# Moving the sums of two convolution tiles behind the normalised pieces of the next layer's input

## The chip, the core and the metric

The kernel runs on one core of a Trainium2 chip. The metric is the device time of one execution in microseconds (us), as a median of several runs. The engines are named as in the profile: PE (matrix multiplications; PEld is its loading of weights), DVE (vector), ACT (scalar and activation), POOL (general purpose) and SP (here it only issues DMAs). Each engine works off its own queue in order; an instruction whose input isn't there yet holds up all that stand behind it on its engine.

## The reference, cut to what matters

Eight images of 32x32 positions ("tokens", 1024 per image) with 256 channels, all in float32. The first layer adds to each image a 3x3 convolution (192 output channels) beside a small attention with relative positions (64 channels). The second layer is a full attention over the 1024 tokens, then a mixture-of-experts layer.

```python
x = x + _L0_conv_ref(_gn(x), ...)        # conv 3x3 -> 192 channels, attention -> 64 channels
t = _to_tokens(x)
t = t + _L1_attn_ref(_ln_t(t), ...)      # _ln_t normalises each token: (v - m) / sqrt(s + eps)
t = t + _L1_ffn_ref(_ln_t(t), ...)
```

What matters here are the sums that the convolution adds to `x`, and the adds `t + ...` and normalised pieces `_ln_t(t)` at the start of the second layer.

## The kernel before, in words

The images go one after the other through the first two stages: `conv_layer_attention(b, ...)` is the first layer's attention of image b, `attention_layer(b, ...)` the second layer's. The mixture of experts follows for all images at the end and isn't touched. An image lies in SBUF as `T[b]`, 128 partitions by 8 pieces of tokens (NT = 8) by 256 channels.

**The convolution** is computed by a short-filter transform: DVE makes six differences `gdif` of the normalised image, PE multiplies them with six transformed filters `convw`, and sums of the products give four neighbouring output columns. `conv_steps` (L517) is a generator: one step is one matmul at L531; 12 steps make a tile `pc` of PSUM with a pair of products; there are three pairs for each of two halves of the image, so 72 steps and six tiles per image. At the end of a tile ACT copies `pc` to SBUF (`m`, L540, two buffers), and POOL turns the pair into sums and adds them to `T`: pair 0 takes two adds into `sd` (L546, L547) and two adds into `T` (L550, L554); pair 1 has, besides, two multiplications on ACT, of one half of `sd` by 2 (L549) and of `sd` by 4 (L552); pair 2 is a single add (L543).

**The seam** is the start of `attention_layer(b)`, where the second layer of image b begins and the first layer of image b+1 is prepared. It normalises the eight pieces of image b in two groups of four (q = 0, 1). Per piece, DVE makes `n` (L815, two buffers), PE transposes it twice into `tpn` (L819), and POOL adds `n` to `T[b]` (L820); n's buffer is free again when both have read it. Between the pieces `fill` takes steps of `input_steps(b+1)`, the next image's projections: its small matmuls `prel` (L484) of 32 rows, the copies of those by DVE (L496) and ACT (L498), and its transposes `tpw` (L509), copied by ACT (L513) and DVE (L511). Each of these steps also names a number of convolution steps, which `conv.run` issues: four are run ahead of the seam and 20 in it, so exactly two tiles, pair 0 and pair 1 of the first half, end in a seam. In POOL's order the first tile's sums stand between the adds of the first and the second piece, the second tile's between those of the sixth and the seventh. After a group, ACT copies the transposes to `nT` (L823). Then come the second layer's projections `pq` (L834), its scores and the rest; POOL adds the bias `bo` to the whole of `T[b]` (L928) after the second tile of scores, and L919 is the first to read that.

There are seven seams with a convolution in them (image 1 to 7 as next image); in the last image's there is none. Image 0's whole convolution runs in `conv_layer_attention`.

**Order.** `tc.manual_schedule` fixes the order of PE and POOL to the program's order in this part. The order on ACT, DVE and SP is set by the scheduler, which places instructions by their estimated times, the program's order breaking ties; so an instruction can stand in ACT's queue at another place than in the program's text.

```python
conv.run(products)                 # in fill(), between the pieces
...
fill(1000.0)                       # all steps that are left
conv.whole()                       # fill up a tile that has been begun
```

Of the kernel before, what the change touches and what calls it, by code (L numbers as in the profile page):

```python
# [10 lines left out]
FP = mybir.dt.float32  # L11
I32 = mybir.dt.int32
AF = mybir.ActivationFunctionType
ALU = mybir.AluOpType
# [3 lines left out]
P = 128  # L18
# [7 lines left out]
CO = C - DK  # L26
# [10 lines left out]
def kernel(  # L37
# [26 lines left out]
    nc = tc.nc  # L64
# [27 lines left out]
    with ExitStack() as ph:  # L92
        wp = ph.enter_context(tc.tile_pool(name="wp", bufs=1))
        work = ph.enter_context(tc.tile_pool(name="work", bufs=1))
# [38 lines left out]
        def st_tile(name):  # L133
            return ps_st["st"].tile([P, 512], FP, tag="st", name=name)
# [80 lines left out]
        def f_tile(name):  # L215
            return work.tile([P, 2, 4, 512], FP, tag="F", name=name, bufs=3)
# [184 lines left out]
        def input_steps(b, held):  # L401
# [112 lines left out]
                yield 0.86, 0  # L514
            held["units"] = [Unit(0, kq, rh, rwd)]

        def conv_steps(b, place):  # L517

            n = 3 * KC
            for r in range(2):
                four = T[b][:, 4 * r : 4 * r + 4, 0:CO]
                for pair in range(3):
                    pc = place[0]("pc")[:, 0 : 2 * CO].rearrange("p (v o) -> p v o", v=2)
                    for v in range(2):
                        for i in range(n):
                            dy, kc = divmod(i, KC)
                            at = (16 * r + dy) * NQ  # L530
                            nc.tensor.matmul(  # L531
                                pc[:, v, :],
                                lhsT=gflat[:, 2 * pair + v, kc, at : at + P],
                                rhs=convw[:, 2 * pair + v, dy, kc * CO : (kc + 1) * CO],
                                start=i == 0,
                                stop=i == n - 1,
                            )
                            if v and i == n - 1:
                                m = work.tile([P, 2, CO], FP, tag="m", name="m", bufs=2)
                                nc.scalar.copy(m, pc)  # L540
                                add = nc.gpsimd.tensor_tensor
                                if pair == 2:
                                    add(four[:, 0:4:3], four[:, 0:4:3], m, ALU.add)  # L543
                                else:
                                    sd = work.tile([P, 2, CO], FP, tag="sd", name="sd")
                                    add(sd[:, 0], m[:, 0], m[:, 1], ALU.add)  # L546
                                    add(sd[:, 1], m[:, 0], m[:, 1], ALU.subtract)  # L547
                                    if pair:
                                        nc.scalar.mul(sd[:, 1], sd[:, 1], 2.0)  # L549
                                    add(four[:, 0:2], four[:, 0:2], sd, ALU.add)  # L550
                                    if pair:
                                        nc.scalar.mul(m, sd, 4.0)  # L552
                                        sd = m
                                    add(four[:, 2:4], four[:, 2:4], sd, ALU.add)  # L554
                            yield

        class Unit:


            def __init__(self, n, kq, rh, rwd):  # L560
                self.g, self.half = divmod(n, 2)
                g, cols = self.g, slice(self.half * 512, self.half * 512 + 512)
                self.rh = rh[g][:, cols]


                self.F = f_tile("F")
                for a in range(2):
                    for hl in range(HG):
                        r = 32 * ((hl + 2 * a) % HG)
                        h = g * HG + hl  # L570
                        nc.sync.dma_start(
                            out=self.F[r : r + 16, a],
                            in_=rh[g][a * 64 + hl : a * 64 + 64 : HG, cols].unsqueeze(1).to_broadcast([16, 4, 512]),
                        )
                        nc.sync.dma_start(
                            out=self.F[r + 16 : r + 24, a],
                            in_=kq[DK + h * DH : DK + (h + 1) * DH, cols].unsqueeze(1).to_broadcast([DH, 4, 512]),
                        )
                for a in range(2):
                    for hl in range(HG):  # L580
                        r = 32 * ((hl + 2 * a) % HG)
                        nc.sync.dma_start(
                            out=self.F[r + 24 : r + 32, a],
                            in_=rwd[g].rearrange("(e j h) s -> h j e s", e=4, h=HG)[hl, :, :, cols],
                        )
                self.mx = work.tile([P, 4, HG], FP, tag="mx", name="mx", bufs=2)
                self.pts = {}
                self.po = None
# [88 lines left out]
            def settle(self, at):  # L677

                pa = st_tile("pa")
                for i in range(4):  # L680
                    nc.tensor.transpose(pa[:, i * P : (i + 1) * P], self.os[:, i * P : (i + 1) * P], ident)
                pav = pa.rearrange("p (i h c) -> p i h c", i=4, h=HG)
                rc = work.tile([P, 4, HG, 1], FP, tag="rc", name="rc", bufs=2)
                nc.vector.reciprocal(rc, pav[:, :, :, DH : DH + 1])
                nc.vector.tensor_tensor(
                    at[:, self.half * 4 : self.half * 4 + 4, self.g * 32 : self.g * 32 + 32].rearrange(
                        "p i (h d) -> p i h d", d=DH
                    ),
                    pav[:, :, :, 0:DH],
                    rc.to_broadcast([P, 4, HG, DH]),  # L690
                    ALU.mult,
                )
# [105 lines left out]
        def attention_layer(b, fill, conv, maxima):  # L798
# [24 lines left out]
                    nc.scalar.copy(nT[:, kc, q * 512 : (q + 1) * 512], tps[kc].rearrange("p j t -> p (j t)"))  # L823
            fill(1000.0)
            conv.whole()

            qkv = f_tile("qkv").rearrange("p a e s -> p (a e s)")
            qk = [qkv[:, i * S : (i + 1) * S] for i in range(2)]
# [116 lines left out]
            m = mv2[:, b]  # L945
# [33 lines left out]
        class Conv:  # L979


            def __init__(self, b):
                self.place = [po_tile]
                self.steps = conv_steps(b, self.place)
                self.left = 2 * NV * 3 * KC if b < B else 0

            def run(self, n):
                n = min(n, self.left)
                for _ in range(n):
                    next(self.steps)  # L990
                self.left -= n

            def whole(self):

                self.run(self.left % (6 * KC))
# [17 lines left out]
        with tc.manual_schedule(engines={mybir.EngineType.PE, mybir.EngineType.Pool}):  # L1013
            conv = Conv(0)
            means = []
            for b in range(B):
# [33 lines left out]
                conv = following  # L1050

                def fill(us):

                    while us > 0:
                        took, products = next(steps, (None, None))
                        if took is None:
                            break
                        us -= took
                        conv.run(products)

                def maxima(s):
                    if not last:
                        pair(held["units"], s, held["rwq"])

                means.append((b, *attention_layer(b, fill, conv, maxima)))
                del T[b]
            token_mean(*means.pop())
# [4 lines left out]
    work = ctx.enter_context(tc.tile_pool(name="fwork", bufs=2))  # L1072
# [21 lines left out]
    def sm(shape, name):  # L1094
        return small.tile(shape, FP, tag=name, name=name)
# [40 lines left out]
    for k in range(TOPK):  # L1136
        m = sm([B, 1], f"m{k}")
# [213 lines left out]
```

## Time and profile before

| | |
|---|---|
| median of 3 runs | 2393.74 us (2389.73 to 2403.38) |
| the profiled execution, its own time | 2405.51 us |
| its span in the profile | 2403.7 us |
| mean granted TensorE clock | 0.962 |
| PE busy | 2315.2 us (96%), 17273 instructions |
| DVE, ACT, POOL busy | 1474.8, 1028.8, 475.3 us |
| copy m (L540) | 48 times, 0.48 us |
| POOL adds L546 and L547 | 32 times each, 0.59 us |
| POOL adds L550 and L554 | 32 times each, 1.00 us |
| ACT multiplications L549 and L552 | 16 times each |
| POOL add of n (L820) | 64 times, 0.73 us |

How to read the views: a line of the timeline has the start in us from the span's begin, the length, the engine, the line of the kernel, the operation, the tiles (output <- inputs) with their shapes, and how many instructions are merged; in brackets stands the time that the engine sat idle before it and who released it. A line of the waits has who waited at which line, for whom, the us in total, the times and the longest. A line of a stretch has the stretch, its length, then the busy us and number of instructions of PE, PEld, DVE, ACT and POOL, then the granted TensorE clock (1.00 is full), the mean busy share of the DMA engines and their GB/s.

### The profile page before, as it was taken

The numbers are of one execution on the slowest core, as the hardware profiler recorded it, in microseconds if no ns is written. First come the engines' busy times: TensorE is split into PE (matmuls) and PEld (weight loads), VectorE is DVE, ScalarE is ACT, GpSimd is POOL, SyncE is SP. The second block draws the span as 40 slices with busy tenths as digits, with TensorE's granted clock in tenths as the row PEclk, the third lists the DMA queues.
The fourth block names the chain that finished last, engine by engine and source line by source line (L and its number), as shares of the span: only waits on it lengthen the run. The fifth ranks groups of instructions, "written<-read, shape, count | busy, mean of one in ns | idle before, by whom it ended". The sixth has DMA issues, their size and how long they took to land. (4 is left out here: it accounts for less than half of the span.)

```text
span 2403.7 us, 41841 instructions
## 1 busy us (share of the span) xinstructions
PE 2315.2 (96%) x17273; PEld 1326.5 (55%) x17273; DVE 1474.8 (61%) x2645; ACT 1028.8 (43%) x1717; POOL 475.3 (20%) x446
## 2 busy tenths in 40 slices
PE   6999999999999999999999999999998789999998
PEld 5535753664366436743773376347633556666665
DVE  7776487558756774677477737773773524444443
ACT  2355335434543463356326632663355322222332
POOL 3202130213021202210230023002301032222231
PEclk7999999899989998999899989998998989999999
DMA  3521252225122503250325033403430122122210
GB/s 107 100 44 30 39 101 37 42 37 102 25 52 38 104 12 58 36 108 3 59 54 91 3 58 73 72 6 55 79 48 2 58 88 70 70 71 71 83 48 27
DMA packets 71469, 135.84 MB, mean 57 GB/s; under 512 B 12000, under 2 KB 24168, under 8 KB 69232
## 3 DMA queue, kind: packets, MB, share of 16 engines
q1 hardware_dynamic: 65488, 115.47, 24.6%
q0 software_dynamic: 3056, 15.73, 2.0%
q8 instruction: 137, 2.24, 0.4%
q10 hardware_dynamic: 2736, 1.97, 0.3%
q14 instruction: 52, 0.43, 0.1%
HBM read 53.43 MB, written 25.17 MB: 33 GB/s over the span
## 5 line engine op out<-in xcount | busy, mean ns | idle before, releaser
L607 DVE TENSOR_REDUCE my<-lg 128x32 f32<-128x1024 f32 x512 | 617.3, 1222 | 173.2 <-PE st L639 125.8
L647 ACT ACTIVATE PT<-st 128x512 f32<-128x512 f32 (+1 forms) x944 | 541.5, 633 | 306.6 <-PE st L639 302.2
L639 PE MATMUL st<-F,km 32*128 32x512 f32 x2048 | 546.4, 643 | 14.2 <-DMA F<-mb 8.9
L599 PE MATMUL lg<-km,F 24*128 24x512 f32 x2048 | 503.6, 636 | 1.8 <-DMA F<-kq 1.8
L656 PE MATMUL po<-PT,vall 128*32 128x256 f32 (+1 forms) x3200 | 315.6, 454 | 2.4 <-ACT PT L647 2.4
L531 PE MATMUL pc<-convw,gdif 128*128 128x192 f32 x1152 | 249.6, 363 | 0.7 <-ACT convw L296 0.7
L656 PEld LDWEIGHTS po<-PT,vall 128*32 128x32 f32 x3200 | 67.0, 108 | 314.9 <-issue 281.7
L599 PEld LDWEIGHTS lg<-km,F 24*128 24x128 f32 x2048 | 143.8, 183 | 163.6 <-issue 124.3
L531 PEld LDWEIGHTS pc<-convw,gdif 128*128 128x128 f32 x1152 | 202.8, 206 | 55.8 <-issue 31.1
L639 PEld LDWEIGHTS st<-F,km 32*128 32x128 f32 x2048 | 178.0, 184 | 92.1 <-issue 48.3
L1281 PE MATMUL py<-w,hT 128*128 128x256 f32 x1024 | 223.6, 379 | 0.0
L1264 PE MATMUL phd<-n2T,w 128*128 128x512 f32 x512 | 223.6, 594 | 0.0
L1281 PEld LDWEIGHTS py<-w,hT 128*128 128x128 f32 x1024 | 194.6, 190 | 33.3 <-issue 7.7
L327 POOL TENSOR_TENSOR T<-T,l0b 128x2048 f32<-128x2048 f32 x8 | 36.3, 4539 | 628.8 <-PE tpx L320 628.8
L1264 PEld LDWEIGHTS phd<-n2T,w 128*128 128x128 f32 x512 | 97.0, 191 | 114.8 <-issue 107.6
L1288 DVE TENSOR_TENSOR r<-py,n 128x256 f32<-128x256 f32 x64 | 27.1, 424 | 213.2 <-PE py L1281 213.1
L1271 ACT ACTIVATE hT<-phd,b1c 128x512 f32<-128x512 f32 x128 | 86.3, 686 | 96.3 <-PE phd L1264 96.1
L872 PE MATMUL lg<-qkv 128*128 128x512 f32 x256 | 121.1, 595 | 0.0
L881 DVE TENSOR_REDUCE nm<-lg 128x1 f32<-128x1024 f32 x64 | 78.1, 1221 | 67.5 <-PE lg L872 67.5
L903 PE MATMUL po<-pt,qkv 128*128 128x256 f32 x512 | 116.5, 380 | 0.0
L820 POOL TENSOR_TENSOR T<-T,n 128x256 f32<-128x256 f32 x64 | 47.3, 755 | 344.1 <-DVE n L815 344.1
L903 PEld LDWEIGHTS po<-pt,qkv 128*128 128x128 f32 x512 | 96.7, 190 | 28.4 <-issue 11.0
(250 smaller groups left out, 2594.7 us busy)
## 6 DMA issues: line engine op xcount, KB each, us to landing
F<-rh SPq DMA_DIRECT2D x256, 128.0 KB
F<-kq SPq DMA_DIRECT2D x256, 64.0 KB
F<-rwd SPq DMA_DIRECT2D x256, 64.0 KB
w<-in_L_ffn_W_dram SPq DMA_DIRECT2D x32, 512.0 KB
rwd<-rw SPq DMA_DIRECT2D x16, 512.0 KB
Td<-T POOLq DMA_DIRECT2D x8, 1024.0 KB, 4.2
T<-Td SPq DMA_DIRECT2D x8, 1024.0 KB
out_dram<-yo SPq DMA_DIRECT2D x16, 512.0 KB
```

What stands on the lines that cost most here:

```text
L531: nc.tensor.matmul(pc[:, v, :], lhsT=gflat[:, 2 * pair + v, kc, at : at + P], rhs=convw[:, 2 * pair + v, dy, kc * CO : (kc + 1) * CO], sta ...
L599: nc.tensor.matmul(lg[:, a, :], lhsT=self.F[r : r + 24, a, 0, i * P : (i + 1) * P], rhs=KM[self.g][r : r + 24, a].rearrange("p e k -> p (e ...
L607: nc.vector.tensor_reduce(my[:, :, hl], lg.rearrange("p a (y x) -> p y a x", y=WW), AX.XY, ALU.max)
L639: nc.tensor.matmul(st[:, i, :] if len(heads) > 1 else st, lhsT=KM[self.g][r : r + 32, a, e, :], rhs=self.F[r : r + 32, a, e, :], start=Tru ...
L647: nc.scalar.activation(self.pts[j][:, hs, :], st, AF.Exp)
L656: nc.tensor.matmul(self.po[32 * hl : 32 * hl + 32, cols], lhsT=vall[:, j, h * (DH + 1) : h * (DH + 1) + 32], rhs=self.pts[j][:, hl, cols], ...
L872: nc.tensor.matmul(lg[:, h, :], lhsT=qk[0][:, i * P : (i + 1) * P], rhs=qk[1][:, h * 512 : (h + 1) * 512], start=True, stop=True,)
L881: nc.vector.tensor_reduce(nm, lg, AX.X, ALU.max, negate=True)
L903: nc.tensor.matmul(po[:, 0:IB], lhsT=v1[:, jc, :], rhs=pt[:, jc, :], start=jc == 0, stop=jc == NT - 1)
L1264: nc.tensor.matmul(phd, lhsT=ws[k][0][:, kc, f * P : (f + 1) * P], rhs=n2T[:, kc, q * 512 : (q + 1) * 512], start=kc == 0, stop=kc == KC - 1,)
L1271: nc.scalar.activation(hT[:, k * NF + f, :], phd, AF.Gelu, bias=b1c[:, f, k * B + b : k * B + b + 1])
L1281: nc.tensor.matmul(py, lhsT=hT[:, k * NF + f, j * P : (j + 1) * P], rhs=ws[k][1][:, f, :], start=k == 0 and f == 0, stop=k == TOPK - 1 and ...
```

## The change

The sums move out of `conv_steps` into a function `sums`. `Conv` gets a second entry in `place`: a list for images 1 to 7, `None` for image 0. While it is a list, the end of a tile makes the copy `m` as before but only notes the sums. The new `settle`, called in `attention_layer` behind `conv.whole()`, issues the noted sums in their order and sets the entry to `None`, so that the image's later tiles issue their sums at once, as before.

```diff
+        def sums(four, pair, m):
+            add = nc.gpsimd.tensor_tensor
+            if pair == 2:
+                add(four[:, 0:4:3], four[:, 0:4:3], m, ALU.add)
+                return
+            sd = work.tile([P, 2, CO], FP, tag="sd", name="sd")
+            add(sd[:, 0], m[:, 0], m[:, 1], ALU.add)
+            add(sd[:, 1], m[:, 0], m[:, 1], ALU.subtract)
+            if pair:
+                nc.scalar.mul(sd[:, 1], sd[:, 1], 2.0)
+            add(four[:, 0:2], four[:, 0:2], sd, ALU.add)
+            if pair:
+                nc.scalar.mul(m, sd, 4.0)
+                sd = m
+            add(four[:, 2:4], four[:, 2:4], sd, ALU.add)
...
                                 nc.scalar.copy(m, pc)
-                                add = nc.gpsimd.tensor_tensor
-                                if pair == 2:
-                                    add(four[:, 0:4:3], four[:, 0:4:3], m, ALU.add)
+                                if place[1] is None:
+                                    sums(four, pair, m)
                                 else:
-                                    sd = work.tile([P, 2, CO], FP, tag="sd", name="sd")
...
+                                    place[1].append((four, pair, m))
...
             fill(1000.0)
             conv.whole()
+            conv.settle()
...
-                self.place = [po_tile]
+                self.place = [po_tile, [] if b else None]
...
+            def settle(self):
+                for left in self.place[1]:
+                    sums(*left)
+                self.place[1] = None
```

More of the change, by code (lines that the diff above doesn't have):

```diff
@@ L540, in conv_steps @@
                                 nc.scalar.copy(m, pc)
-                                add = nc.gpsimd.tensor_tensor
-                                if pair == 2:
-                                    add(four[:, 0:4:3], four[:, 0:4:3], m, ALU.add)
-                                else:
-                                    sd = work.tile([P, 2, CO], FP, tag="sd", name="sd")
[L546 to L554, printed above, removed]
+                                if place[1] is None:
+                                    sums(four, pair, m)
+                                else:
+                                    place[1].append((four, pair, m))
                             yield
```

## The prediction

> **What bounds the kernel now.** I read the page first: PE is busy 96% of the span, DVE 61%, ACT 43%, POOL 20%. So TensorE is the bound, and an edit on POOL and ACT counts only where PE waits for it or where PE runs slower because of it. Hence the waits next:
>
> ```profile
> DVE n L815 <- POOL T L820: 20.5, 17, 2.0
> ...
> PE tpn L819 <- DVE n L815: 14.7, 11, 5.7
> ```
>
> PE waits for normalised pieces n, and DVE in turn waits for POOL's adds at L820, which give back the two buffers of n. Asked seam by seam, the second line is one wait of 1.02 to 1.03 us in each of the seven seams (7.1 us) plus the last image's, where no convolution is left. Now the third seam on POOL's timeline:
>
> ```profile
> 697.26 0.60 POOL L546 TENSOR_TENSOR sd<-m 128x192 f32<-128x192 f32 x1 [4.28 <-ACT m L540]
> ...
> 700.40 1.41 POOL L820 TENSOR_TENSOR T<-T,n 128x256 f32<-128x256 f32 x2
> ```
>
> POOL reaches the sums of the first convolution tile, waits 4.28 us there for the tile to end, works 3.14 us on four adds, and only then frees n. The PE timeline of the same seam:
>
> ```profile
> 694.21 0.38 PE L819 MATMUL tpn<-ident,n 128*128 128x128 f32 x2
> 694.52 1.24 PE L484 MATMUL prel<-kq,bdw 32*64 32x32 f32 x64
> 695.70 0.92 PE L531 MATMUL pc<-convw,gdif 128*128 128x192 f32 x4
> 696.45 0.38 PE L819 MATMUL tpn<-ident,n 128*128 128x128 f32 x2
> ...
> 702.02 0.44 PE L819 MATMUL tpn<-ident,n 128*128 128x128 f32 x2 [1.02 <-DVE n L815]
> ...
> 706.30 1.93 PE L484 MATMUL prel<-kq,reld 32*64 32x32 f32 x64
> 708.16 1.65 PE L531 MATMUL pc<-convw,gdif 128*128 128x192 f32 x4
> 709.61 0.63 PE L819 MATMUL tpn<-ident,n 128*128 128x128 f32 x2
> ...
> 717.61 7.03 PE L834 MATMUL pq<-nT,wqkv 128*128 128x512 f32 x16
> ```
>
> The stall is the small part. From start to start, ahead of it 64 prel take 1.18 us and four pc 0.75; behind it 1.86 and 1.45. The stretches (their column PEclk is the third from the right) say why:
>
> ```profile
> 701.00:703.00 2.00, 0.98 (x44) 0.82 (x46) 1.21 (x3) 0.62 (x2) 1.77 (x4) 1.00 0.90 327
> 703.00:706.00 3.00, 3.00 (x44) 2.82 (x36) 1.40 (x2) 1.04 (x2) 1.28 (x2) 0.52 0.21 39
> ```
>
> Directly behind the stall the clock is halved, and it stays so until 716.8, four steps of 3.41 us (every change of clock in this trace is a multiple of that). So it goes in all seven seams. Last, what ACT holds at a seam's end:
>
> ```profile
> 716.20 0.36 ACT L549 ACTIVATE sd<-sd 128x192 f32<-128x192 f32 x1 [1.31 <-POOL sd L547]
> 716.49 1.01 ACT L513 COPY rwq<-tpw 128x1024 f32<-128x1024 f32 x1
> 717.40 0.53 ACT L552 ACTIVATE m<-sd 128x384 f32<-128x384 f32 x1
> 717.82 1.06 ACT L823 COPY nT<-tpn 128x512 f32<-128x512 f32 x2
> ```
>
> The second tile's two multiplications (L549, L552) stand in ACT's queue ahead of the copies of nT, which the projections pq read.
>
> **What the change moves.** Per seam: six POOL adds of 128x192 or 128x384 and two more (0.59 and 1.0 us each, 3.14 us for tile 0, about as much for tile 1 plus its waits for ACT) and the two ACT multiplications (0.36 and 0.53). No DMA is among them, and the seam's own DMA issues on SP (F, rwd) neither read nor write what they touch. Nothing is added. On POOL they pass the seven L820 adds behind tile 0's place and two behind tile 1's; the copy m stays where it was, so the PSUM tile is freed as before. m has two buffers and exactly two tiles end in a seam; the next comes tens of microseconds later: no cost.
>
> **Gain, the stall.** Without the sums the fourth piece's buffer is free before 697 (its predecessor's transposes end at 696.83), so DVE can make it right behind its copy of prel, at 699.2; PE wants it at 701.0. The stall of 1.02 goes.
>
> **Gain, the clock.** Here a rule speaks against the change. The Trainium skill ("TensorE: Matmul & The Clock Gate", section "Why this matters for your kernels") puts the fall to half clock on PE gaps over some 3 us, a whole idle window. By that rule a gap of 1.02 us can't be the cause, the half clock would come from the mix of small matmuls and stay, and the change would be worth 7 x 1.02 = 7.1 us. I cut the trace into its 3.41 us steps. In the seams 7 of 7 steps with 1.01 to 1.03 us idle are followed by half clock, and the three steps ahead of each, same mix without idle time, by none (0 of 21). Elsewhere between 80 and 1840 us, 1.0 us idle (waits of L639 for a DMA of mb, among full transposes) leads to it in 0 of 7, 0.75 us in 2 of 7, 2.0 us in the one case. So short gaps can do it, in this mix of 32-row matmuls above all, and I go by the rows: no gap, no fall.
>
> What the seam then costs at full clock, from 701.0 to pq: 5 pairs tpn at 0.31 = 1.55; 3 prel at 1.18 = 3.54; pc of 6, 4 and 6: 0.75, and twice 0.75 + 2 x 0.18 (eight take 1.41), 2.97; 2 groups of eight tpw at 0.88 (the eight tp of L892 at full clock) = 1.76. Sum 9.82 where 16.61 stood: 6.8 us per seam, 1.0 of stall and 5.8 of clock. The seven seams lie within 16.5 and 16.7, so 7 x 6.8 = 47.5 us.
>
> **Cost, the new place.** POOL can begin the sums when the last L820 is done. At full clock its n comes at 706.3 (0.1 behind the sixth piece's transposes), that add ends at 707.5, tile 0's sums at 710.6 (+3.14), tile 1's two adds of m at 711.75 (+1.14; its m is ready by 709.3). Then ACT's L549 can run, 711.75 to 712.1. PE meanwhile reaches pq at 710.8 and after two matmuls (7.03/16 = 0.44 each), at 711.7, needs the second half of nT: copies L823, ready to run at 710.7. All hangs on ACT's order. That is not the program's but a planner's (L552 is traced ahead of L513 and runs behind it). What its clockwork thinks, the trace shows only by bounds. If L823 is ahead of L549, nothing waits: cost 0. If L549, L513, L552 come first as today, L823 starts behind 712.1 + 0.95 + 0.48 = 713.5, its first half is there at 714.0, and PE stands 2.3 us. Which? In today's order L549 was ready for the planner by the time that L513 was, at latest one L549 later. On the chip that fits half clock (716.20 against 716.3), at full clock L513 would be ready 0.95 sooner. So the planner's PE is as slow against its POOL as the half-clock rows. With these, tile 1 ends 3.94 us behind the sixth piece's transposes (which give the eighth its buffer), and L513 is ready 2.27 later, at 6.2, L823 at 6.8; POOL's chain is 0.6 + 0.73 + 3.14 + 1.14 = 5.6. L549 comes first. I take 2.3 us. Bounds: 0, and 3.2 should POOL's adds stretch by a third.
>
> A stall of 2.3 us invites the clock again. A half-clock step costs 5.8/13.65 x 3.41 = 1.4 us. Bounds: none (the gap may be cut by two steps, and pq is dense) to four steps (5.8 us, the seam's own duration); I take one in three seams of four, 1.1, since the falls in dense stages (433, 1365, 1819 us) lasted one step each.
>
> **The rest.** POOL's 4.5 us add of bo (L928) queues behind the sums; it would end near 719 against 724.98 today, and its first reader (L919) runs at 742.2: over 15 us of cover by PE's scores. Without that cover each us late would be a us on PE. Sharing between DVE and POOL: n takes 0.41 alone and up to 0.80 beside POOL; it moves to other copies; between -0.4 and +0.4 per seam, hidden under PE, taken as 0. The three single falls elsewhere shift with the phase of the steps: -4 to +6 us in all, taken as 0.
>
> **Sum.** 6.8 - 2.3 - 1.1 = 3.4 per seam, 24 us. The profiled execution took 2405.5 (span 2403.7 and 1.8 around it), 0.5% above the median of 2393.7; the saving is in us per seam, so it comes off either: 2382 there, **2370** in the median.
>
> **Rivals.**
> 1. Full cover (0.27): the planner puts L823 ahead of the multiplications. No new gap: 2393.7 - 47.5 = 2346. For it: on the chip L823 is ready 1 us sooner. Against: the planner's ratio above.
> 2. The clock falls anyway (0.13): the mix, or some other short wait of the faster seam, halves it. Then PE is late again and ACT's wait is hidden; the stall alone goes: 2387. The rule speaks for it, the 0 of 21 against.
> 3. Slower (0.10): the gap ahead of pq halves the clock, and it doesn't come back in one step but stays through the projections and first scores of the second layer, as it stays four steps in the seam today. The saving of 6.8 - 2.3 = 4.5 is used up by 3.2 steps; with five, each seam loses 2.5: 2411. Against: that stage's matmuls have 128 rows and up to 512 columns, and today's half clock ends in the very step in which the full transposes tpw begin.
>
> My own case has 0.50, from 2358 (no falls, shorter gap) to 2383. Faster by over 0.5%, about what a measurement of this kernel can tell from no change, needs less than 2381.8: 0.27 + 0.43 = 0.70; same 0.19, slower 0.11. Range for 8 in 10: 2342 to 2392, which leaves out the slower rival and the best of rival 1.
>
> **What would show it.** Right: no wait of tpn for n in seams 1 to 7, POOL's L820 without the 4.28 us ahead, PEclk 1.00 from the first tpn to the last. The second part: a wait of PEld or PE at pq for ACT's nT of about 2.3 us, with ACT L549 waiting for POOL ahead of L513, and a single half step behind it. Rival 1 shows L823 ahead of L549 and no wait. Rival 2 shows 0.50 in the seam with no gap before it; rival 3 shows 0.50 in the second layer's scores. I am wrong at the root if the gap at the fourth piece stays, because DVE then waits for something other than L820.

## The result, and the profile after

The changed kernel takes 2362.06 us (median of 4 runs, 2361.41 to 2362.31), before it was 2392.38 (4 runs, 2389.73 to 2403.38): a ratio of 0.9864, 95% interval 0.9833 to 0.9895. It is faster by 1.4%, in the forecast's range of 2342 to 2392 and 8 us under its value of 2370. The profiled execution itself went from 2405.51 to 2361.41 us, span 2403.7 to 2359.6, mean granted clock 0.962 to 0.983.

First PE's waits after the change. The changed file has the same lines at other numbers: L815 is now L823, L820 L828, L823 L831, L834 L843; the moved multiplications L549 and L552 are L527 and L530.

```profile
PE pq L843 <- ACT nT L831: 9.7, 7, 1.4
...
PE tpn L827 <- DVE n L823: 7.2, 4, 5.4
```

The last line is now the last image's alone: four waits instead of eleven, none in a seam with a convolution. The first line is new: seven waits for nT, one per seam, of at most 1.4 us. On the third seam's POOL timeline all eight adds of n come first and the sums stand behind them in one block:

```profile
683.87 0.73 POOL L828 TENSOR_TENSOR T<-T,n 128x256 f32<-128x256 f32 x1 [1.50 <-DVE n L823]
686.12 0.73 POOL L828 TENSOR_TENSOR T<-T,n 128x256 f32<-128x256 f32 x1 [1.51 <-DVE n L823]
...
692.83 0.72 POOL L828 TENSOR_TENSOR T<-T,n 128x256 f32<-128x256 f32 x1 [1.40 <-DVE n L823]
693.51 0.60 POOL L524 TENSOR_TENSOR sd<-m 128x192 f32<-128x192 f32 x1
...
701.63 4.52 POOL L937 TENSOR_TENSOR T<-T,bo 128x2048 f32<-128x2048 f32 x1
```

PE in the same seam, from the fourth piece (687.26) on:

```profile
687.26 0.38 PE L827 MATMUL tpn<-ident,n 128*128 128x128 f32 x2
687.57 1.13 PE L484 MATMUL prel<-kq,reld 32*64 32x32 f32 x64
688.63 1.24 PE L549 MATMUL pc<-convw,gdif 128*128 128x192 f32 x6
...
696.48 1.88 PE L843 MATMUL pq<-nT,wqkv 128*128 128x512 f32 x4
699.74 5.42 PE L843 MATMUL pq<-nT,wqkv 128*128 128x512 f32 x12 [1.38 <-ACT nT L831]
705.00 1.96 PE L881 MATMUL lg<-qkv 128*128 128x512 f32 x4
```

687.26 has no idle time in brackets, and 64 prel keep to 1.13 us where they took 1.93. The granted clock of the stretches stays at 1.00 through the seam and through the new wait:

```profile
687.00:690.00 3.00, 3.00 (x77) 2.60 (x75) 1.10 (x2) 1.58 (x3) 0.73 (x1) 1.00 0.87 279
690.00:693.00 3.00, 3.00 (x129) 2.75 (x130) 0.83 (x2) 0.08 (x1) 0.90 (x2) 1.00 0.73 137
693.00:696.00 3.00, 3.00 (x42) 2.94 (x35) 0.69 (x1) 0.97 (x2) 2.92 (x5) 1.00 0.91 121
...
698.00:700.00 2.00, 0.62 (x2) 0.26 (x2) 0.69 (x1) 2.00 (x4) 1.00 (x1) 1.00 0.77 131
```

From the stall's start at the fourth piece to the first scores (lg) a seam took 23.44 to 23.54 us before and takes 17.73 to 17.75 now: 5.71 to 5.80 less in each of the seven, 40.2 us. That leaves 3.9 of the profiles' 44.1. Single steps of half clock between the seams, at 433 and 1365 us before and at 880 us after, make some 1.6 of it. The seam's first three pieces make 1.1: they take 6.78 us before, where the idle time follows them, and 6.62 after. The rest lies around the last image's seam; its cause is open. ACT's queue shows whom the new wait is for:

```profile
697.94 0.36 ACT L527 ACTIVATE sd<-sd 128x192 f32<-128x192 f32 x1 [2.89 <-POOL sd L525]
698.21 0.99 ACT L513 COPY rwq<-tpw 128x1024 f32<-128x1024 f32 x1
699.10 1.08 ACT L831 COPY nT<-tpn 128x512 f32<-128x512 f32 x2
700.06 0.55 ACT L530 ACTIVATE m<-sd 128x384 f32<-128x384 f32 x1
```

ACT stands 2.89 us at the multiplication L527, waiting for POOL's late sums, with the ready copies of tpw and nT behind it.

### The profile page after: what moved, and what is told of

The parts are those of the page before. It is cut to its first block, busy times and chain, and to the rows that moved or that the text cites. A ratio compares the mean times of both kernels' runs of the same rounds, so it can differ in the third digit from the quotient of the medians.

```text
span 2359.6 us, 41847 instructions
## 1 busy us (share of the span) xinstructions
PE 2269.0 (96%) x17273; PEld 1285.9 (54%) x17273; DVE 1470.0 (62%) x2645; ACT 1028.5 (44%) x1717; POOL 475.4 (20%) x446
## 5 line engine op out<-in xcount | busy, mean ns | idle before, releaser
L549 PE MATMUL pc<-convw,gdif 128*128 128x192 f32 x1152 | 230.1, 343 | 0.7 <-ACT convw L296 0.7
L549 PEld LDWEIGHTS pc<-convw,gdif 128*128 128x128 f32 x1152 | 187.8, 193 | 55.3 <-issue 31.1
L828 POOL TENSOR_TENSOR T<-T,n 128x256 f32<-128x256 f32 x64 | 47.3, 747 | 402.2 <-DVE n L823 395.9
```

Of the source, the lines that this page charges most:

```text
L549: nc.tensor.matmul(pc[:, v, :], lhsT=gflat[:, 2 * pair + v, kc, at : at + P], rhs=convw[:, 2 * pair + v, dy, kc * CO : (kc + 1) * CO], sta ...
```

## The experiments

The theory: a seam lost its time through one gap of 1.0 us that halved the clock for four steps; the change takes the gap away, and its price is ACT's wait for POOL. The rivals: the half clock came from the sums beside PE's small matmuls, or from the mix alone; the new wait is of the copies themselves; putting off the second tile is part of the gain.

In the later sittings the kernel before came to a median of 2399.4 (23 runs, then 55, 2384.52 to 2413.82) and 2400.1 (7 runs), above the first sitting's 2392.38. Ratios below are against the runs of the same sitting; the changed kernel itself wasn't run again, so a difference to its 2362.06 is one between sittings, and the traces are the firmer ground there.

**The kernel before once more.** No edit.

> The kernel of before, unchanged, for a second profile. The profiled execution of before took 2405.5 us, the unprofiled median is 2392.4, and the saving in the profiles is 44 us where that of the medians is 30. Theory A (the 1.0 us gap halves the clock by chance of the 3.41 us steps): in an execution near 2391 two or three of the seven seams escape the half clock, each worth 5.8 us, while the gap of 1.02 us stays in all seven. Theory B (the difference is elsewhere, for instance in the last stage): all seven seams fall again and the difference lies outside them. Ratio 1.00 by both.

Measured 2398.23 (20 runs, 2385.39 to 2404.89), ratio 0.9989 (0.997 to 1.0008). The profiled execution, at 2402.92, again has its half clock of four steps in all seven seams, so of an execution with fewer falls there is no trace. But the granted clock is known of each run: the fastest, 2385.39, had 0.973, the slowest, 2404.89, 0.961. One four-step fall lowers the mean by 13.65 x 0.5 / 2400 = 0.0028, so the two lie some four falls apart, 4.9 us each. That fits theory A without showing in which seams; shorter falls would fit as well, and one such is in the trace of the second half alone below. Nor are falls in seams the only scatter: the changed kernel spreads over 0.9 us, but the kernel of the next run, whose trace has no fall in a seam either, over 7.

**Three buffers for n, sums in their old place.**

```diff
-                    n = work.tile([P, C], FP, tag="n", name="n", bufs=2)
+                    n = work.tile([P, C], FP, tag="n", name="n", bufs=3)
...
-                    self.my = work.tile([P, WW, HG], FP, tag="my", name="my", bufs=2)
+                    self.my = work.tile([P, WW, HG], FP, tag="my", name="my", bufs=1)
```

> The kernel of before with three buffers for n instead of two (room made by one buffer instead of two for my, which only DVE touches); the sums stay where they were. Theory A, the gap at the fourth piece halves the clock: the gap goes, since the fourth piece takes the first piece's buffer, which POOL frees ahead of the sums, and with it the half clock of the seam; 6.8 us per seam less a wait at pq of at most 0.7: 2392 - 43 to 48 = about 2347. Theory B, the half clock comes from POOL's sums running beside PE's small matmuls, or from the mix: it stays although the gap goes, 7 x 1.0 = 7 us, about 2385.

Measured 2356.45 (2352.05 to 2359.14), ratio 0.981 (0.9766 to 0.9854). Its waits, and the fourth piece of a seam:

```profile
PE tpn L819 <- DVE n L815: 5.4, 1, 5.4
...
PE pq L834 <- ACT nT L823: 1.5, 7, 0.2
```

```profile
685.47 0.38 PE L819 MATMUL tpn<-ident,n 128*128 128x128 f32 x2
685.78 1.13 PE L484 MATMUL prel<-kq,reld 32*64 32x32 f32 x64
```

The sums run where they always ran, beside the same small matmuls, and no seam falls to half clock. That clears the sums and the mix: the gap was the cause. The time is 9 us over theory A's 2347, but that number was reckoned from a base of 2392: against the same sitting's 2399.4 the saving is 43 us, the low end of its 43 to 48. The waits at pq (0.2 us on PE, up to 1.0 on its loading of weights) still cost something: from the first pq to the first scores a seam takes 7.35 us here, 6.87 in the next run, where they are gone.

**The multiplications on POOL.** In the changed kernel, for the settled sums alone:

```diff
-        def sums(four, pair, m):
+        def sums(four, pair, m, late=False):
...
-                nc.scalar.mul(sd[:, 1], sd[:, 1], 2.0)
+                if late:
+                    nc.gpsimd.tensor_scalar(sd[:, 1], sd[:, 1], 2.0, None, ALU.mult)
+                else:
+                    nc.scalar.mul(sd[:, 1], sd[:, 1], 2.0)
...
-                nc.scalar.mul(m, sd, 4.0)
+                if late:
+                    nc.gpsimd.tensor_scalar(m, sd, 4.0, None, ALU.mult)
+                else:
+                    nc.scalar.mul(m, sd, 4.0)
...
-                    sums(*left)
+                    sums(*left, late=True)
```

> The changed kernel with the two multiplications of the settled sums on POOL instead of ACT, so that ACT's copies of nT stand behind nothing that waits for POOL. Theory A: the wait of pq for nT (7 x 1.38 = 9.7 us) is the multiplication's place in ACT's queue; it goes, 2362 - 9.7 = about 2352, and POOL's longer chain (some 1.5 us) stays under the 15 us before the first reader of the bias add. Theory B: the nT copies are late by themselves (the copy of tpw ahead of them, 1 us): the wait stays at 1 us or more and the time at 2360 or more.

Measured 2350.12 (2349.37 to 2350.67), ratio 0.9781 (0.9737 to 0.9824), 12 us under the changed kernel. ACT's queue in a seam, and PE's projections:

```profile
694.29 1.02 ACT L513 COPY rwq<-tpw 128x1024 f32<-128x1024 f32 x1 [0.54 <-PE tpw L509]
695.20 1.08 ACT L837 COPY nT<-tpn 128x512 f32<-128x512 f32 x2
```

```profile
695.18 7.03 PE L849 MATMUL pq<-nT,wqkv 128*128 128x512 f32 x16
```

The copies now wait for PE only, and the 16 matmuls of pq run in one piece. The wait was the place of L527 in ACT's queue, not the copies.

**One half of the change each.** First the first tile alone put off, then the second alone:

```diff
-                                if place[1] is None:
+                                if place[1] is None or pair:
...
+                                if place[1] is None or not pair:
```

> One half of the change: only the first tile's sums are put off, the second tile's are issued where it ends, as before. Theory A (the whole gain is the first tile's place, the second tile's move is what costs): no gap at the fourth piece, no half clock, and ACT's multiplications are ready earlier, so that pq waits 0.2 to 0.5 us instead of 1.38: about 2355, faster than the whole change. Theory B (both moves are needed, the second tile's sums hold up the seventh and eighth piece when PE runs at full clock): a new wait of PE for n at the eighth piece and a half clock there, 2365 to 2390.

> The other half of the change: only the second tile's sums are put off. Theory A: nothing is gained, the gap of 1.0 us and the half clock stay in all seams, and at half clock PE comes to pq too late to notice ACT's queue: as before, 2392 to 2400. Theory B: the second tile's move has a gain of its own, since the seventh and eighth piece come earlier: 2380 or less.

The first alone: 2353.29 (2351.75 to 2355.16), ratio 0.9795 (0.9751 to 0.9839), 9 us faster than the whole change. No gap, no fall in a seam, and pq waits 0.2 us, since the multiplications are ready 2 us behind the tile's end. The second alone: 2399.4 (20 runs, 2383.96 to 2406.43), ratio 1.0001 (0.9979 to 1.0023), with the gap and the fall in all seven seams. The whole gain is the first tile's; moving the second costs and gives nothing.

The seventh seam of the second half alone is an exception that no theory foresaw. Its three steps of 3.41 us from the gap on:

```profile
1634.35:1637.76 3.41, 2.38 (x73) 1.88 (x71) 1.75 (x3) 1.16 (x3) 3.18 (x5) 1.00 0.87 305
1637.76:1641.18 3.42, 3.42 (x44) 3.00 (x47) 1.18 (x3) 0.58 (x1) 1.00 (x3) 0.50 0.35 87
1641.18:1644.59 3.41, 3.41 (x114) 3.14 (x109) 1.03 (x2) 0.00 (x0) 1.19 (x2) 1.00 1.03 118
```

The full clock is back after one step, not four, in the same mix with PE as busy as elsewhere, and the seam is some 4.6 us shorter than the other six. So a gap of 1.0 us doesn't always cost four steps; what let this one end is open.

**A gap made on purpose.** The changed kernel with idle adds on POOL at the first tile's old place (their result is used by nothing), five as shown, and six and four in two more runs:

```diff
+                                    if pair == 0:
+                                        gap = work.tile([P, 2, CO], FP, tag="sd", name="gap")
+                                        for _ in range(5):
+                                            nc.gpsimd.tensor_tensor(gap[:, 0], m[:, 0], m[:, 1], ALU.add)
```

> The changed kernel with five idle adds of 128x192 on POOL (into a scratch tile, they change no result) at the first tile's old place, 2.75 us instead of the sums' 3.14: a gap of about 0.45 us at the fourth piece. Theory A (the gap's size in a step of 3.41 us decides): 0.45 us is under half of what the seam had, the clock stays full in all or nearly all seams: 2362 + 7 x 0.45 = about 2365. Theory B (any gap in this mix halves the clock): it falls in all seven seams and hides the wait at pq, 2362 + 7 x (0.45 + 5.8 - 1.38) = about 2396.

> The same with six adds, 3.3 us: a gap of about 1.0 us at the fourth piece, as before the change, though the sums themselves are moved away. Theory A (the gap halves the clock): it falls in all or nearly all seams, and PE is late enough to hide the wait at pq: 2362 + 7 x (1.0 + 5.8 - 1.38) = about 2400, the time of before. Theory B (the sums themselves, not the gap, were the cause): the clock stays full, 2362 + 7 x 1.0 = about 2369.

> The changed kernel with four idle adds on POOL at the first tile's old place. Five gave a gap of 1.12 us (0.65 us each, not 0.55), so four give about 0.45 us. Theory A (in this mix a step of 3.41 us tolerates a little under 1.0 us of idle time): no seam falls, each costs its gap: 2362 + 7 x 0.45 = about 2365. Theory B (any gap there halves the clock): 2362 + 7 x 4.9 = about 2396.

Five adds took 3.29 us (0.65 each, not 0.55), so their gap was 1.12 us, not the small one that was meant. They measured 2405.07 (20 runs, 2400.83 to 2409.59), ratio 1.0019 (1.0003 to 1.0035). Six made a gap of 1.8 us: 2409.71 (2393.15 to 2416.97), ratio 1.0035 (1.0016 to 1.0054). With the sums moved away, the gap alone brings back the whole time of before. Four made 0.46 us: 2370.14 (2365.06 to 2375.73), ratio 0.9884 (0.9842 to 0.9926), no fall in any seam. That is theory A, though its 2365 is only the lowest of the four runs; the profile has two single falls between the seams, one more than that of the changed kernel. Two seams of PE, the first of the run with five adds, the second of that with four:

```profile
697.57 0.44 PE L831 MATMUL tpn<-ident,n 128*128 128x128 f32 x2 [1.12 <-DVE n L827]
697.94 1.88 PE L484 MATMUL prel<-kq,reld 32*64 32x32 f32 x64
701.83 0.63 PE L831 MATMUL tpn<-ident,n 128*128 128x128 f32 x2
```

```profile
691.99 0.44 PE L831 MATMUL tpn<-ident,n 128*128 128x128 f32 x2 [0.46 <-DVE n L827]
694.50 0.38 PE L831 MATMUL tpn<-ident,n 128*128 128x128 f32 x2
```

After 1.12 us the next pair of transposes comes 4.3 us later at half speed, after 0.46 us it comes 2.5 us later at full speed. One seam of the run with five adds escaped. Its gap of 1.12 us was cut by the edge between two steps: 0.98 us idle in the first (3.41 less 2.43 busy), 0.14 in the second.

```profile
465.95:469.37 3.42, 2.43 (x72) 1.90 (x71) 1.28 (x2) 1.06 (x1) 3.14 (x5) 1.00 0.61 237
469.37:472.78 3.41, 3.28 (x106) 2.88 (x106) 2.07 (x5) 1.66 (x3) 2.24 (x3) 1.00 0.39 101
```

The other six had 1.07 to 1.13 us in one step and fell. That speaks for the idle time within a step as what counts, on the evidence of one seam.

**A longer wait at pq.** Two idle adds ahead of the settled sums:

```diff
                 for left in self.place[1]:
+                    if left[1] == 0:
+                        gap = work.tile([P, 2, CO], FP, tag="sd", name="gap")
+                        for _ in range(2):
+                            nc.gpsimd.tensor_tensor(gap[:, 0], left[2][:, 0], left[2][:, 1], ALU.add)
                     sums(*left)
```

> The changed kernel with two idle adds on POOL (1.1 us, no result depends on them) ahead of the settled sums, so that the wait of pq for nT grows from 1.38 to about 2.5 us, near what the prediction took. Theory A, the prediction's: a gap of that size halves the clock for one step in about three seams of four, also among dense matmuls: 2362 + 7 x (1.1 + 1.1) = about 2377. Theory B: among matmuls of 128 rows and 512 columns such a gap leaves the clock full, and it costs its own length: 2362 + 7 x 1.1 = about 2370.

Measured 2376.76 (2375.13 to 2380.08), ratio 0.9896 (0.9837 to 0.9955). The wait was 2.72 us, 1.34 more, and three of the seven seams fell to half clock, for four steps in all. 7 x 1.34 + 4 x 1.4 = 15 us, as measured (14.7). Neither theory fits as stated. Cut by steps of 3.41 us: the three seams with 2.05, 2.19 and 2.45 us idle in one step fell, the four with 1.42 to 1.76 didn't. One step of each kind, the second seam's and the third's:

```profile
473.95:477.37 3.42, 1.66 (x4) 0.38 (x2) 1.89 (x2) 0.84 (x2) 2.87 (x5) 1.00 0.76 113
...
702.65:706.06 3.41, 0.96 (x3) 0.13 (x1) 1.20 (x2) 1.53 (x3) 2.76 (x4) 1.00 0.69 106
706.06:709.47 3.41, 3.14 (x4) 1.50 (x5) 0.00 (x0) 1.13 (x3) 2.21 (x2) 0.50 0.53 70
```

So the matmuls of pq tolerate nearly twice the idle time of the seam's mix.

**Both waits taken away, nothing put off.** The three buffers with the multiplications of the seam's tile on POOL:

> The kernel of before, sums in their old place, with three buffers for n and the multiplications of the seam's second tile on POOL. Theory A (a seam costs only its two waits of PE, whichever way they are taken away): no gap at the fourth piece, no wait at pq, as in the changed kernel with the multiplications on POOL: 2350, within 4 us. Theory B (putting the sums off has a worth of its own, for instance since POOL and DVE work less side by side): 2356 or more.

Measured 2348.36 (2347.49 to 2350.49), ratio 0.9794 (0.9757 to 0.9832): the same as the 2350.12 of the put-off sums with those multiplications. That is theory A: from the fourth piece to the first scores most seams take 16.09 us in both traces, so taking away the two waits is all that the put-off sums do for a seam. This and the multiplications on POOL are the fastest versions, 12 to 14 us under the changed kernel; the three buffers alone and the first half alone beat it by 6 and 9.

## Why the prediction was right, step by step

*The stall at the fourth piece* (1.0 us, gone): right, in all seven seams.

*The clock* (a gap of 1.0 us halves it; without the gap no fall): right, and the step that decided the case. The Trainium skill's rule ("TensorE: Matmul & The Clock Gate", section "Why this matters for your kernels"), which ties the fall to gaps of about 3 us, is contradicted here: gaps of 1.02 to 1.13 us within one step were followed by half clock in 27 of 27 seams (7 each of before, its repetition and the second half alone, 6 of the run with five adds), those of 1.4 to 1.8 us with six adds in 7 of 7. (The forecast's lowest, 1.01, is 1.02 by the exact edges of its step.) Three buffers for n took the gap away and left the sums, and the fall was gone; idle adds brought the gap back without the sums, and the fall was back. By the rule the change would have been worth 7 us, by the rows 47 less the new wait; it brought 40 in the seams.

*The seam at full clock* (9.82 us): measured 9.22. The second half of the prel takes 1.07 us from start to start, not the 1.18 of the first half's, and tpn ahead of tpw 0.22, not 0.31. The saving so far is 16.6 - 9.2 = 7.4, not 6.8.

*The new wait at pq* (2.3 us): right in kind, in place and in its reason, L527 ahead of the copies; 1.38 in size. Three terms were off. PE was taken to need the second half of nT after two matmuls; a product is two rows in the trace, so it needs it after four, 0.9 us later. The planner put L530 behind the copies, not ahead of them, 0.5 us. The other way, PE came to pq 1.46 us ahead of L527 (696.48 and 697.94), not 0.95, since its seam was shorter: 2.3 - 0.9 - 0.5 + 0.5 = 1.4. That the planner would put L527 ahead of L513 came true; whether it did so for the reason given, a slow PE against POOL, no run shows.

*The clock at the new wait* (1.1 us per seam): wrong, 0 of 7 fell. The wait was shorter than forecast, and up to 1.76 us idle in a step no seam fell. For a wait of the forecast's size the term was less far off: with 2.72 us three of seven fell, for four steps in all, some 0.8 us per seam.

*Sum*: 5.7 us per seam, not 3.4. That the median still came within 8 us of the forecast is in part luck. In the profiles the saving is 44 us against 24 forecast; in the medians it is 30, and against the 2399.4 of the later sittings it would be 37. In the later sittings the faster runs of before have a higher granted clock, so less half clock to lose, and three of the four that stand for before here were faster than most of those. The forecast's sentence that the saving "comes off either" was wrong: it depends on how often, and for how long, the clock falls.

*The rest* (the bias add's cover, DVE and POOL side by side): nothing waits for L937; it ends at 706.2 us and its first reader starts at 722.7, so the cover of over 15 us was there. What POOL and DVE side by side cost, put at nothing, no run isolates.

## What to carry to other kernels

Look for a clock column that drops behind a short wait before pricing the wait: here 1 us of idle time and the half clock behind it cost some 7. When work is moved behind other work on one engine, list what the other engines do for it: two small multiplications on ACT, not the eight adds on POOL, were the price of this change, and keeping them off the queue that PE waits for gave 12 us more. Try the smallest part first; half of this edit, or one more buffer of 1 KB per partition (paid for with a second buffer elsewhere), gave more than the whole.

## What the runs showed of the hardware

In each of the twelve traces all changes of the granted clock lie on one grid of 3.41 us. A short idle time of PE within one such step can halve the clock, and how much it takes depends on what runs there. Among 32-row matmuls, convolution matmuls and transposes, 1.02 us or more did it in all 34 seams, and 0.98 (one seam) and 0.46 us in none. Among matmuls of 128 rows and 512 columns up to 1.76 us did it in none, and from 2.05 in all three. It isn't the idle time alone: in the attention of the first layer steps with the same 0.75 us idle fell in some cases and not in others (2 of 7 before, 1 of 7 after).

How long the half clock lasts varies too. In 33 of those 34 seams the mix, with PE busy without a break, didn't bring the full clock back for three steps or more, and it came back behind the step in which the transposes tpw began; in one it was back after a single step, without them. Why the mix counts, and what ends the half clock, these runs don't show.
